# Layer 1 of a four-layer convolution stack: the residual folded into the convolution's weights, and the results' statistics taken on ScalarE

## The chip, the cores and the metric

One core of a Trainium2 chip runs the whole program. The time is device microseconds of one execution; a kernel's time is the median of its runs. The profile is one more execution, recorded by the hardware profiler. It is somewhat longer than the timed runs.

## The reference

Four layers run one after the other on x of 4 images, 64 channels, 256 x 256 points, in float32. Each is x + f(gn(x)), where gn normalises groups of two channels over the image. The change touches layer 1, whose f is a plain 3x3 convolution:

```python
def _gn(v, G=32, eps=1e-5):
    B_, C_, H_, W_ = v.shape
    g = v.reshape(B_, G, C_ // G, H_, W_)
    m = jnp.mean(g, axis=(2, 3, 4), keepdims=True)
    s = jnp.var(g, axis=(2, 3, 4), keepdims=True)
    return ((g - m) / jnp.sqrt(s + eps)).reshape(v.shape)

# --- layer 1 (conv_preact) ---
x = x + _L1_conv_ref(_gn(x), L1_conv_kernel)   # 3x3, 64 -> 64 channels, padding 1
```

Layer 0 is a gated depthwise convolution with 8x8 Fourier patches, layer 2 a convolution that chooses between two results point by point, layer 3 a Fourier filter. Each layer needs the mean and variance of the whole image that the layer before wrote, so each layer also collects statistics of its own results for the next.

## The kernel before

Layers run in order; between them x goes through device memory (one tensor for each image). Each layer is written as a loop over steps in which the order of the instructions on TensorE (PE), VectorE (DVE), ScalarE (ACT) and SyncE (SP, which issues the loads) is the order in which the code calls its functions (the block `manual_schedule`); GpSimd (POOL) issues the stores. At the seams between layers a scheduler may move the first work of the next layer ahead.

Layer 1 (`_layer1`, from L727) works in 64 steps: 4 images times 16 stretches of 16 rows. In a step n:

- `load` (L750) brings 2 x 10 rows: partitions 0 to 63 hold the channels of the upper 8 rows with a row on each side, partitions 64 to 127 those of the lower 8. The buffers of x come from `slot`, two for even and two for odd steps, so four in all.
- `normalize` (L772) writes gn(x) = r * x + nb with one ScalarE operation (L236) into one of two buffers xn. r (1/std) and nb (-mean/std) are known for each channel and image.
- `transform` (L788) forms four row combinations of xn on VectorE (L802). The convolution is a fast one along the rows: two output rows come from four products (index 0 to 3) instead of six.
- `product` (L804) computes product i on TensorE: for each of three column taps four matmuls of 64x64 weights with 512 points (L809), the four quarters of the array beside each other. Products 0 and 3 also add the residual, unnormalised x, with the identity matrix as weights (L817). The weights are `wk` for products 0 and 3, and `wg`, half the sum (or difference) of the three row taps, for 1 and 2.
- `fetch` (L822) copies product 1 from PSUM to SBUF on ScalarE (L824); `middle` (L826) forms product 1 plus and minus product 2 on VectorE (L830); `result` (L832) adds product 0 or 3 to these into the output tile o (L836, "o1", three buffers).
- `finish` (L840) takes bn_stats of o on VectorE (L849, four of 128x512 each step) and stores o (L852). After the last stretch of an image, `group_norm_parts` (L173) turns the statistics into r and nb of layer 2 in small pieces, one piece a step (`next_norms`): bn_aggr (L180), a matmul over the channel groups, a few small VectorE operations, a second matmul, a power on GpSimd.

The PSUM tiles of the products rotate over four buffers. Loads run three steps ahead, normalising two, transforming one; `finish` lies one step behind. The main loop reads:

```python
load(n + 3)
product(n, 1); fetch(n); product(n, 2)
finish(n - 1)
transform(n + 1, 1, 2); middle(n)
product(n, 0); result(n, 0)
transform(n + 1, 0, 3); normalize(n + 2)
product(n, 3); result(n, 3)
```

At the end of layer 1, layer 2 (`_layer2`, from L894) reuses the slots for its x and xn: its first normalised tiles are the input of its first convolve (L1044), which also needs constants (peri, thr, scl, wc) whose memory layer 1 held.

Of the kernel before, what the change touches and what calls it, by code (L numbers as in the profile page):

```python
# [10 lines left out]
F32 = mybir.dt.float32  # L11
U32 = mybir.dt.uint32
AF = mybir.ActivationFunctionType
ALU = mybir.AluOpType
# [3 lines left out]
C = 64  # L18
# [100 lines left out]
class _Net:  # L119
# [49 lines left out]
    def group_norm(self, *args):  # L169
        for _ in self.group_norm_parts(*args):  # L170
            pass

    def group_norm_parts(self, n, b, bst, avg=None):  # L173

        same, moved = avg or (self.avg, self.avg)
        nc, sp = self.nc, self.sp
        mv = sp.tile([128, 2], F32, tag="mv", name=f"mv{n}_{b}")
        nc.vector.bn_aggr(mv, bst.rearrange("p n s -> p (n s)"))  # L180
        yield
        ps = self.small(f"gn{n}_{b}")
        nc.tensor.matmul(ps[:, 0:1], same, mv[:, 0:1], start=True, stop=True)
        if moved is not same:
            nc.tensor.matmul(ps[:, 1:2], moved, mv[:, 0:1], start=True, stop=True)
        gm = sp.tile([128, 1], F32, tag="gm", name=f"gm{n}_{b}")
        nc.vector.tensor_copy(gm, ps[:, 0:1])
        d = sp.tile([128, 1], F32, tag="gd", name=f"gd{n}_{b}")
        nc.vector.tensor_sub(d, mv[:, 0:1], gm)
        q = sp.tile([128, 1], F32, tag="gq", name=f"gq{n}_{b}")  # L190
        nc.vector.scalar_tensor_tensor(q, d, d, mv[:, 1:2], ALU.mult, ALU.add)
        if moved is not same:
            nc.vector.tensor_copy(gm, ps[:, 1:2])
        yield
        ps2 = self.small(f"gv{n}_{b}")
        nc.tensor.matmul(ps2[:, 0:1], moved, q, start=True, stop=True)
        v = sp.tile([128, 1], F32, tag="gv", name=f"gvs{n}_{b}")
        nc.vector.tensor_scalar(v, ps2[:, 0:1], EPS, None, ALU.add)
        r, nb = self.r[n][:, b : b + 1], self.nb[n][:, b : b + 1]
        nc.gpsimd.tensor_tensor(r, v, self.mhalf, ALU.pow)  # L200
        nc.vector.scalar_tensor_tensor(nb, gm, -1.0, r, ALU.mult, ALU.mult)
# [525 lines left out]
    def _layer1(self, ctx, src, dst):  # L727
        tc, nc, a, B, H, W = self.tc, self.nc, self.a, self.B, self.H, self.W
        pool = lambda name, bufs, **k: ctx.enter_context(tc.tile_pool(name=name, bufs=bufs, **k))
        cp, p_t = pool("l1c", 1), pool("l1t", 2)  # L730
        p_s, p_o, pp = pool("l1s", 2), pool("l1o", 3), pool("l1p", 1, space=PSUM)
        turn = count()

        def pair(name):

            return pp.tile([128, 2, 512], F32, tag=f"p{next(turn) % 4}", name=name)

        self.small = lambda name: pair(name)[:, 0, :]
        rows2 = lambda t: t.rearrange("p s (r w) -> p s r w", r=2)
        W1 = W + 1  # L740
        halves = [slice(0, C), slice(C, 128)]

        xns = [self.slot(2, f"xn1_{k}")[:, 0:10] for k in range(2)]
        for t in xns:
            nc.gpsimd.memset(t[:, :, 0 : W + 2 : W1], 0.0)
        its = [(b, r0) for b in range(B) for r0 in range(0, H, 16)]
        NI = len(its)
        xt, ts, ms, sums, outs, bst = {}, {}, {}, {}, {}, {}

        def load(n):  # L750
            if n >= NI:
                return
            b, r0 = its[n]
            x = xt[n] = self.slot(n % 2, f"x1_{n}")[:, 0:10, 0:W]
            for s in range(2):
                top = r0 + 8 * s - 1
                i0, i1 = max(0, -top), min(10, H - top)
                nc.sync.dma_start(x[halves[s], i0:i1], src[b][:, top + i0 : top + i1, :])
# [7 lines left out]
        gs = [wk[:, 0]] + [cp.tile([128, 3, C], F32, name=f"wg{k}") for k in range(2)] + [wk[:, 2]]  # L766
        side = cp.tile([128, 3, C], F32, name="wside")
        nc.vector.tensor_add(side, wk[:, 0], wk[:, 2])
        for g, op in ((gs[1], nc.vector.tensor_add), (gs[2], nc.vector.tensor_sub)):
            op(g, side, wk[:, 1])  # L770
            nc.vector.tensor_scalar(g, g, 0.5, None, ALU.mult)  # L771
        def normalize(n):  # L772
            if n >= NI:
                return
            b, r0 = its[n]
            x, xn = xt[n], xns[n % 2]
            i0, i1 = 0, 10
            if r0 == 0:
                i0 = 1
                nc.gpsimd.memset(xn[0:C, 0, 1:W1], 0.0)  # L780
                self.normalize(xn[C:128, 0, 1:W1], x[C:128, 0], 1, b, C, 128)
            if r0 + 16 == H:
                i1 = 9
                nc.gpsimd.memset(xn[C:128, 9, 1:W1], 0.0)
                self.normalize(xn[0:C, 9, 1:W1], x[0:C, 9], 1, b, 0, C)
            self.normalize(xn[:, i0:i1, 1:W1], x[:, i0:i1], 1, b)

        def transform(n, *which):  # L788
            if n >= NI:
                return  # L790
            xn = xns[n % 2]
            if n not in ts:
                ts[n] = p_t.tile([128, 4, 4, W + 2], F32, tag="t", name=f"t_{n}")
            d = [xn[:, k : k + 7 : 2] for k in range(4)]
            for i in which:
                p, q, op = (
                    (d[0], d[2], nc.vector.tensor_sub),
                    (d[1], d[2], nc.vector.tensor_add),
                    (d[2], d[1], nc.vector.tensor_sub),
                    (d[3], d[1], nc.vector.tensor_sub),  # L800
                )[i]
                op(ts[n][:, i], p, q)  # L802

        def product(n, i):  # L804
            m = ms[n, i] = pair(f"m{i}_{n}")
            tiles = [(s, j) for s in range(2) for j in range(2)]
            for dx in range(3):
                for s, j in tiles:
                    nc.tensor.matmul(  # L809
                        rows2(m)[halves[j], s], gs[i][halves[s], dx, :],  # L810
                        ts[n][halves[s], i, 2 * j : 2 * j + 2, dx : dx + W],
                        start=(dx == 0), stop=(dx == 2 and i in (1, 2)),
                    )
            if i in (0, 3):
                r = 1 if i == 0 else 2
                for s, j in tiles:
                    nc.tensor.matmul(  # L817
                        rows2(m)[halves[j], s], self.ident[halves[s], halves[s]],
                        xt[n][halves[s], r + 4 * j : r + 4 * j + 3 : 2], start=False, stop=True,
                    )  # L820

        def fetch(n):  # L822
            t = sums[n, 1] = p_s.tile([128, 2, 512], F32, tag="s1", name=f"s1_{n}")
            nc.scalar.copy(t, ms.pop((n, 1)))  # L824

        def middle(n):  # L826
            m1, m2 = sums.pop((n, 1)), ms.pop((n, 2))
            for i, op in ((0, nc.vector.tensor_add), (3, nc.vector.tensor_sub)):
                t = sums[n, i] = p_s.tile([128, 2, 512], F32, tag=f"s{i}", name=f"s{i}_{n}")
                op(t, m1, m2)  # L830
# [9 lines left out]
        def finish(n):  # L840
            if n < 0:
                return
            b, r0 = its[n]
            if b not in bst:
                bst[b] = self.stats_tile(f"bst2_{b}", H * W // 1024)
            o = outs.pop(n)
            for s in range(2):
                for i in (0, 2):
                    nc.vector.bn_stats(bst[b][:, r0 // 4 + i + s, :], o[:, s, i : i + 2].rearrange("p r w -> p (r w)"))  # L849
            v = dst[b][:, r0 : r0 + 16, :].rearrange("c (s j r) w -> j c s r w", s=2, j=2)  # L850
            for j in range(2):
                nc.gpsimd.dma_start(v[j], o[halves[j]])  # L852
            if r0 + 16 == H:
                self.norms.append(self.group_norm_parts(2, b, bst.pop(b)))

        with tc.manual_schedule(
            engines={
                mybir.EngineType.PE, mybir.EngineType.DVE, mybir.EngineType.Activation, mybir.EngineType.SP
            }
        ):  # L860
            for n in range(2):
                normalize(n)
            transform(0, 1, 2, 0, 3)
            for n in range(NI):
                load(n + 3)
                product(n, 1)
                fetch(n)
                product(n, 2)
                finish(n - 1)
                transform(n + 1, 1, 2)  # L870
                middle(n)
                product(n, 0)
                result(n, 0)
                transform(n + 1, 0, 3)
                normalize(n + 2)
                product(n, 3)
                result(n, 3)
                self.next_norms()
                xt.pop(n)
                ts.pop(n)  # L880
            finish(NI - 1)

# [496 lines left out]
```

## Time and profile before

| | before |
|---|---|
| time, median of 3 runs | 7563.33 us (7562.54 to 7565.89) |
| span of the profiled execution | 7617.3 us |
| mean granted TensorE clock | 0.971 |
| TensorE matmul / weight load busy | 7303.1 / 4319.0 us |
| VectorE busy | 6594.7 us |
| ScalarE busy | 3659.3 us |
| GpSimd busy | 660.3 us |
| layer 1, first to last matmul | about 4886 to 5660 us |

A view of groups names a line, an engine, an operation, what is written from what, the shape, how many there were, their busy time and mean duration, and the idle time of that engine just before them with what ended it. A chain of waits follows the end of the program back from each instruction to what released it. A view in order of time merges equal neighbours. Matmuls overlap: four that use different quarters of the array run together, so their durations don't add up.

### The profile page before, as it was taken

What the parts mean: (1) busy time and instruction counts of PE and PEld (TensorE: products, weight loads), DVE (VectorE), ACT (ScalarE), POOL (GpSimd) and SP (SyncE); (2) the same over time, 40 slices, a digit from 0 to 9 for tenths busy, and PEclk for the clock granted to TensorE, in tenths of its full rate; (3) what the DMA queues carried; (4) which work ended last, traced back from release to release, by engine and by line L of the source; (5) the groups of instructions that cost most, each with busy time, mean ns of one, the idle gap of its engine ahead of it and who ended that gap; (6) DMA issues with size and microseconds to landing.
All of it is one profiled execution on the core that took longest, in us unless ns stands there. A gap on an engine that the chain in (4) does not pass through costs nothing. (4 is left out here: it accounts for less than half of the span.)

```text
span 7617.3 us, 398890 instructions
## 1 busy us (share of the span) xinstructions
PE 7303.1 (96%) x189304; PEld 4319.0 (57%) x189304; DVE 6594.7 (87%) x5915; ACT 3659.3 (48%) x3917; POOL 660.3 (9%) x1435
## 2 busy tenths in 40 slices
PE   6999999999999999999999999899989999998797
PEld 4666666666666666666666666433324444443276
DVE  7999999999999999999899899899989888885345
ACT  3445444444444454444444545322238778774111
POOL 0000000000000000000000000001102222221011
PEclk9999999999999999999999999999999999999955
DMA  3222222222222222222111121487766766677789
GB/s 129 62 65 63 63 61 61 59 61 59 61 62 61 59 59 62 62 59 54 45 47 47 46 50 44 100 197 196 195 162 171 178 171 175 171 178 232 243 333 396
DMA packets 651203, 875.63 MB, mean 115 GB/s; under 512 B 44020, under 2 KB 470212, under 8 KB 647524
## 3 DMA queue, kind: packets, MB, share of 16 engines
q1 hardware_dynamic: 568548, 581.61, 28.8%
q0 software_dynamic: 81024, 268.50, 12.1%
q8 instruction: 1485, 24.33, 1.4%
q14 instruction: 146, 1.20, 0.1%
HBM read 581.50 MB, written 268.44 MB: 112 GB/s over the span
## 5 line engine op out<-in xcount | busy, mean ns | idle before, releaser
L462 PE MATMUL psd<-y,diag 32*32 32x512 f32 x73296 | 2547.8, 598 | 16.0 <-issue 14.5
L500 DVE SCALAR_TENSOR_TENSOR v<-y,sb_w_dw,v 128x2048 f32<-128x2048 f32 x1024 | 2391.0, 2335 | 110.3 <-ACT v L498 87.7
L462 PEld LDWEIGHTS psd<-y,diag 32*32 32x32 f32 x73296 | 1524.3, 103 | 877.9 <-issue 366.7
L442 ACT COPY y<-psy 128x512 f32<-128x512 f32 x1536 | 915.4, 659 | 1683.3 <-PE psy L435 1681.2
L400 DVE TENSOR_TENSOR up<-psu,flt 128x768 f32<-128x768 f32 x1024 | 932.4, 951 | 226.6 <-PE psu L397 225.8
L435 PEld LDWEIGHTS psy<-sb_c_bdft,up 64*64 64x64 f32 x49152 | 859.5, 135 | 350.9 <-issue 139.1
L435 PE MATMUL psy<-sb_c_bdft,up 64*64 64x64 f32 x49152 | 931.3, 221 | 32.6 <-issue 29.7
L397 PE MATMUL psu<-win,xf 64*64 64x384 f32 x8192 | 788.5, 487 | 18.5 <-DVE h L482 10.1
L1000 DVE TENSOR_TENSOR q<-xn 128x2313 f32<-128x2313 f32 (+2 forms) x256 | 627.3, 2493 | 1.7 <-ACT xn L236 1.7
L1055 PE MATMUL one<-z,wp 32*32 32x512 f32 x16384 | 592.6, 596 | 20.3 <-issue 15.4
L1001 ACT ACTIVATE q<-q 128x2313 f32<-128x2313 f32 (+2 forms) x256 | 528.9, 2086 | 32.0 <-DVE q L1000 30.7
L476 ACT ACTIVATE h<-psd 128x1024 f32<-128x1024 f32 x258 | 251.3, 1023 | 534.9 <-PE psd L462 534.9
L236 ACT ACTIVATE xn<-x,nb,r 128x1024 f32<-128x1024 f32 (+3 forms) x272 | 488.1, 1798 | 41.5 <-DVE q L1000 23.6
L1055 PEld LDWEIGHTS one<-z,wp 32*32 32x32 f32 x16384 | 366.5, 103 | 228.5 <-issue 87.4
L1014 PE MATMUL div<-q,ones 64*32 64x512 f32 x8192 | 469.0, 597 | 13.6 <-ACT q L1001 9.8
L407 POOL MEMSET y<- 128x22 f32 x384 | 52.2, 137 | 4251.2 <-ACT y L415 3217.2
L397 PEld LDWEIGHTS psu<-win,xf 64*64 64x64 f32 x8192 | 305.6, 134 | 184.6 <-issue 85.2
L1088 POOL DMA_DIRECT2D x<-r x512 | 274.2, 543 | 971.0 <-DVE r L1085 943.6
L809 PE MATMUL m<-t,wk 64*64 64x512 f32 x3072 | 352.5, 588 | 0.0
L809 PE MATMUL m<-t,wg 64*64 64x512 f32 x3072 | 343.5, 591 | 4.5 <-DVE wg L771 4.5
L1014 PEld LDWEIGHTS div<-q,ones 64*32 64x32 f32 x8192 | 153.6, 107 | 321.1 <-issue 256.9
L824 ACT COPY s<-m 128x1024 f32<-128x1024 f32 x64 | 64.8, 1013 | 558.9 <-PE m L809 548.6
(138 smaller groups left out, 7625.2 us busy)
## 6 DMA issues: line engine op xcount, KB each, us to landing
x<-x SPq DMA_DIRECT2D x240, 640.0 KB, 6.3
x<-x SPq DMA_DIRECT2D x122, 1024.0 KB, 10.7
x<-in_x_dram SPq DMA_DIRECT2D x256, 256.0 KB, 3.8
x<-o POOLq DMA_DIRECT2D x128, 512.0 KB, 9.2
r<-x SPq DMA_DIRECT2D x512, 128.0 KB, 4.1
x<-r POOLq DMA_DIRECT2D x512, 128.0 KB, 4.0
out_dram<-x POOLq DMA_DIRECT2D x64, 1024.0 KB, 9.8
r<-in_x_dram SPq DMA_DIRECT2D x248, 256.0 KB, 3.8
```

What stands on the lines that cost most here:

```text
L236: self.nc.scalar.activation(dst, src, AF.Identity, bias=self.nb[n][p0:p1, b : b + 1], scale=self.r[n][p0:p1, b : b + 1])
L397: nc.tensor.matmul(ps[halves[n], s, 0:384], xf[t][halves[s], n, 4 * g + k], win[halves[s]], start=True, stop=True)
L400: nc.vector.tensor_mul(ups[t, g][:, :, k, :], ps[:, :, 0:384], flt.broadcast_to([128, 2, 384]))
L435: nc.tensor.matmul(ps[halves[c], n, s, :, k, :], up[halves[n], s, k, i * 128 + c * C : i * 128 + (c + 1) * C], bdft[halves[n]], start=True ...
L442: nc.scalar.copy(yt[t][i][:, 3:11, w0 : w0 + 64].rearrange("p r (k n w) -> p n r k w", k=4, n=2), ps[:, :, s])
L462: ins = nc.tensor.matmul(d[q // 2][quarters[j], q % 2], diag[quarters[q], i, k, :], rows_in(t, i, quarters[q], j, dy)[:, :, dx : dx + W], ...
L500: nc.vector.scalar_tensor_tensor(v, s, wdw[:, 2, k : k + 1], v, ALU.mult, ALU.add)
L809: nc.tensor.matmul(rows2(m)[halves[j], s], gs[i][halves[s], dx, :], ts[n][halves[s], i, 2 * j : 2 * j + 2, dx : dx + W], start=(dx == 0), ...
L1000: nc.vector.tensor_sub(d, p0, p1)
L1001: nc.scalar.activation(d, d, AF.Square)
L1014: ins = nc.tensor.matmul(ps[quarters[j], h], ones[halves[h]], q[n, g, k][halves[h], r + 2 * j : r + 2 * j + 2, o : o + W], start=(m == 0), ...
L1055: ins = nc.tensor.matmul(rows2(ps[g])[quarters[j], k], w[quarters[i]], z[quarters[i], h, 2 * j + dy : 2 * j + dy + 2, dx : dx + W], tile_p ...
```

## The change

For layer 1 the residual x can be written with the normalised rows: x = std * gn(x) + mean, with std = 1/r and mean = -nb/r. So x + conv(gn(x)) is one convolution whose centre tap has std added on the diagonal, plus a constant for each channel. In the fast convolution the centre row tap lies in products 1 and 2 only: half of std is added to the centre column's weights of product 1 and taken from those of product 2. The constant goes in as a bias where product 1 is fetched. The matmuls with the identity are dropped; so x is no longer held until they have run.

For each image `fold` computes std, mean and the two changed 64x64 weights on VectorE, where that image's first normalize is called.

The statistics of the results move from VectorE (bn_stats) to ScalarE: two passes over o, one for the sum of o and one for the sum of (o - c) squared, c being the mean of the image's first stretch; both write the values themselves to a tile that nobody reads (`junk`). `sums_parts` makes mean and variance of them at the image's end. At the first stretch of an image VectorE computes c from the first sum.

```diff
+    def sums_parts(self, n, b, acc, c, size):
+        def aggregate(mv):
+            t = sp.tile([128, 2], F32, tag="sums", name=f"sums{n}_{b}")
+            nc.vector.tensor_reduce(t, acc.rearrange("p k s -> p s k"), mybir.AxisListType.X, ALU.add)
+            nc.vector.tensor_scalar(t, t, 1.0 / size, None, ALU.mult)
+            nc.vector.tensor_copy(mv[:, 0:1], t[:, 0:1])
+            d = sp.tile([128, 1], F32, tag="sumd", name=f"sumd{n}_{b}")
+            nc.vector.tensor_add(d, t[:, 0:1], c)
+            nc.vector.tensor_mul(d, d, d)
+            nc.vector.tensor_sub(mv[:, 1:2], t[:, 1:2], d)
+        return self.group_norm_parts(n, b, aggregate)
...
+        half = cp.tile([128, C], F32, name="half")
+        for s in range(2):
+            nc.vector.tensor_scalar(half[halves[s]], self.ident[halves[s], halves[s]], 0.5, None, ALU.mult)
+        junk = cp.tile([128, 2, 4, W], F32, name="junk")
+
+        def fold(b):
+            r = self.r[1][:, b : b + 1]
+            t = p_i.tile([128, 2], F32, tag="i", name=f"i_{b}")
+            nc.vector.reciprocal(t[:, 0:1], r)
+            nc.vector.scalar_tensor_tensor(t[:, 1:2], self.nb[1][:, b : b + 1], -1.0, t[:, 0:1], ALU.mult, ALU.mult)
+            w = p_i.tile([128, 2, C], F32, tag="w", name=f"wi_{b}")
+            nc.vector.scalar_tensor_tensor(w[:, 0], half, t[:, 0:1], gs[1][:, 1], ALU.mult, ALU.add)
+            nc.vector.tensor_scalar(w[:, 1], half, t[:, 0:1], None, ALU.mult)
+            nc.vector.tensor_sub(w[:, 1], gs[2][:, 1], w[:, 1])
+            folded[b] = t[:, 1:2], w
+
         def normalize(n):
...
-            x, xn = xt[n], xns[n % 2]
+            x, xn = xt.pop(n), xns[n % 2]
             i0, i1 = 0, 10
             if r0 == 0:
                 i0 = 1
+                fold(b)
...
         def product(n, i):
             m = ms[n, i] = pair(f"m{i}_{n}")
-            tiles = [(s, j) for s in range(2) for j in range(2)]
+            w = [gs[i][:, dx] for dx in range(3)]
+            if i in (1, 2):
+                w[1] = folded[its[n][0]][1][:, i - 1]
             for dx in range(3):
...
-            if i in (0, 3):
-                r = 1 if i == 0 else 2
-                for s, j in tiles:
-                    nc.tensor.matmul(
-                        rows2(m)[halves[j], s], self.ident[halves[s], halves[s]],
-                        xt[n][halves[s], r + 4 * j : r + 4 * j + 3 : 2], start=False, stop=True,
-                    )
 
         def fetch(n):
             t = sums[n, 1] = p_s.tile([128, 2, 512], F32, tag="s1", name=f"s1_{n}")
-            nc.scalar.copy(t, ms.pop((n, 1)))
+            nc.scalar.activation(t, ms.pop((n, 1)), AF.Identity, bias=folded[its[n][0]][0])
...
             o = outs.pop(n)
-            for s in range(2):
-                for i in (0, 2):
-                    nc.vector.bn_stats(bst[b][:, r0 // 4 + i + s, :], o[:, s, i : i + 2].rearrange("p r w -> p (r w)"))
+            k = r0 // 16
+            if k == 0:
+                acc[b] = self.sp.tile([128, H // 16, 2], F32, tag="acc", name=f"acc_{b}")
+            nc.scalar.activation(junk, o, AF.Identity, accum_out=acc[b][:, k, 0:1])
+            if k == 0:
+                acc["c", b] = self.sp.tile([128, 1], F32, tag="accc", name=f"accc_{b}")
+                nc.vector.tensor_scalar(acc["c", b], acc[b][:, 0, 0:1], -1.0 / (8 * W), None, ALU.mult)
+            nc.scalar.activation(junk, o, AF.Square, bias=acc["c", b], accum_out=acc[b][:, k, 1:2])
...
             if r0 + 16 == H:
-                self.norms.append(self.group_norm_parts(2, b, bst.pop(b)))
+                self.norms.append(self.sums_parts(2, b, acc.pop(b), acc.pop(("c", b)), H * W // 2))
...
-                xt.pop(n)
                 ts.pop(n)
```

More of the change, by code (lines that the diff above doesn't have):

```diff
@@ L171, in group_norm @@
             pass
+    def sums_parts(self, n, b, acc, c, size):
+        nc, sp = self.nc, self.sp
+        def aggregate(mv):
[8 more added lines that the diff above has]
+        return self.group_norm_parts(n, b, aggregate)
     def group_norm_parts(self, n, b, bst, avg=None):
@@ L179, in group_norm_parts @@
         mv = sp.tile([128, 2], F32, tag="mv", name=f"mv{n}_{b}")
-        nc.vector.bn_aggr(mv, bst.rearrange("p n s -> p (n s)"))
+        if callable(bst):
+            bst(mv)
+        else:
+            nc.vector.bn_aggr(mv, bst.rearrange("p n s -> p (n s)"))
         yield
@@ L731, in _layer1 @@
         p_s, p_o, pp = pool("l1s", 2), pool("l1o", 3), pool("l1p", 1, space=PSUM)
+        p_i = pool("l1i", 2)
         turn = count()
@@ L747, in _layer1 @@
         NI = len(its)
-        xt, ts, ms, sums, outs, bst = {}, {}, {}, {}, {}, {}
+        xt, ts, ms, sums, outs, acc, folded = ({} for _ in range(7))
         def load(n):
@@ L805, in product @@
             m = ms[n, i] = pair(f"m{i}_{n}")
-            tiles = [(s, j) for s in range(2) for j in range(2)]
+            w = [gs[i][:, dx] for dx in range(3)]
+            if i in (1, 2):
+                w[1] = folded[its[n][0]][1][:, i - 1]
             for dx in range(3):
-                for s, j in tiles:
[L809 to L812, printed above, removed]
-                    )
-            if i in (0, 3):
-                r = 1 if i == 0 else 2
-                for s, j in tiles:
-                    nc.tensor.matmul(
-                        rows2(m)[halves[j], s], self.ident[halves[s], halves[s]],
-                        xt[n][halves[s], r + 4 * j : r + 4 * j + 3 : 2], start=False, stop=True,
-                    )
+                for s in range(2):
+                    for j in range(2):
+                        nc.tensor.matmul(
+                            rows2(m)[halves[j], s], w[dx][halves[s]],
+                            ts[n][halves[s], i, 2 * j : 2 * j + 2, dx : dx + W],
+                            start=(dx == 0), stop=(dx == 2),
+                        )
         def fetch(n):
             t = sums[n, 1] = p_s.tile([128, 2, 512], F32, tag="s1", name=f"s1_{n}")
-            nc.scalar.copy(t, ms.pop((n, 1)))
+            nc.scalar.activation(t, ms.pop((n, 1)), AF.Identity, bias=folded[its[n][0]][0])
         def middle(n):
@@ L843, in finish @@
             b, r0 = its[n]
-            if b not in bst:
-                bst[b] = self.stats_tile(f"bst2_{b}", H * W // 1024)
             o = outs.pop(n)
-            for s in range(2):
-                for i in (0, 2):
-                    nc.vector.bn_stats(bst[b][:, r0 // 4 + i + s, :], o[:, s, i : i + 2].rearrange("p r w -> p (r w)"))
+            k = r0 // 16
[6 more added lines that the diff above has]
+            nc.scalar.activation(junk, o, AF.Square, bias=acc["c", b], accum_out=acc[b][:, k, 1:2])
             v = dst[b][:, r0 : r0 + 16, :].rearrange("c (s j r) w -> j c s r w", s=2, j=2)
```

## The prediction

> **What bounds the kernel now.** I read the chain that ended last, then the groups of layer 1, then the order of time per engine, then the DMA share, then the seam to layer 2. The chain in two steady steps (start us, duration us, what):
>
> ```profile
> 4900.20 7.72 PE m L809 x72
> 4907.92 0.86 PE m L817 x8
> 4908.78 2.57 PE m L809 x24
> 4911.35 0.86 PE m L817 x8
> 4912.21 7.72 PE m L809 x72
> ```
>
> It is TensorE alone. A step (16 rows of the image) takes 4912.21 - 4900.20 = 12.01 us: 96 conv matmuls and 16 residual ones (L817). The trace has two matmul instructions for each call, so L817's x1024 are 64 steps x 8 calls x 2. The two L817 pieces are 2 x 0.86 = 1.72 us of each step. The groups of 4890 to 5650 us (count | busy us, mean ns | idle before and its releaser):
>
> ```profile
> L802 DVE TENSOR_TENSOR t<-xn 128x1032 f32<-128x1032 f32 x251 | 296.6, 1223 | 0.0
> L836 DVE TENSOR_TENSOR o<-m,s 128x1024 f32<-128x1024 f32 x126 | 154.0, 1222 | 14.7 <-PE m L817 14.7
> L849 DVE BATCH_NORM_STATS2 bst<-o 128x6 f32<-128x512 f32 x249 | 153.8, 680 | 1.9
> L830 DVE TENSOR_TENSOR s<-s,m 128x1024 f32<-128x1024 f32 x126 | 147.7, 1213 | 2.9 <-PE m L809 2.9
> L824 ACT COPY s<-m 128x1024 f32<-128x1024 f32 x63 | 63.8, 1013 | 548.6 <-PE m L809 548.6
> L236 ACT ACTIVATE xn<-x,nb,r 128x2560 f32<-128x2560 f32 x55 | 139.3, 2532 | 0.0
> ```
>
> VectorE hardly waits, so it is the close second; ScalarE waits most of the time. One step of VectorE in order of time (the bracket is idle before), then ScalarE's wait in a step:
>
> ```profile
> 5205.30 2.36 DVE L802 TENSOR_TENSOR t<-xn 128x1032 f32<-128x1032 f32 x2
> 5207.58 2.34 DVE L830 TENSOR_TENSOR s<-s,m 128x1024 f32<-128x1024 f32 x2
> 5210.24 1.23 DVE L836 TENSOR_TENSOR o<-m,s 128x1024 f32<-128x1024 f32 x1 [0.32 <-PE m L817]
> 5214.93 2.47 DVE L849 BATCH_NORM_STATS2 bst<-o 128x6 f32<-128x512 f32 x4
> 5217.32 2.36 DVE L802 TENSOR_TENSOR t<-xn 128x1032 f32<-128x1032 f32 x2
> ```
>
> ```profile
> 5216.30 1.01 ACT L824 COPY s<-m 128x1024 f32<-128x1024 f32 x1 [8.58 <-PE m L809]
> ```
>
> From start to start: a transform costs 1.14 us (2.28 for two), the four bn_stats 5217.32 - 5214.93 = 2.39. The stretch as a whole (busy of PE, PEld, DVE, ACT, POOL; then granted clock, DMA share, GB/s):
>
> ```profile
> 4886.00:5652.00 766.00, 766.00 (x7108) 274.56 (x7112) 742.04 (x777) 220.71 (x135) 78.95 (x140) 1.00 0.79 192
> ```
>
> TensorE is full at full clock, VectorE 97% busy, DMA 79%. SyncE's waits say why loads are not earlier: a buffer of x is held until the residual matmul has read it.
>
> ```profile
> SPq L758 <- PE m L817: 651.7, 60, 24.2
> ```
>
> Last, the seam:
>
> ```profile
> 5665.02 10.32 DMA x<-x
> 5675.37 0.05 issue
> 5675.42 2.53 ACT xn L236
> 5677.95 0.04 issue
> 5677.99 4.76 PE psz L1044 x23
> ```
>
> Layer 1's matmuls end near 5660.2; layer 2's first convolve runs from 5677.99, 17.8 us later, behind a load that had waited for an x buffer held by L817.
>
> **What the Trainium skill says.** (1) "ScalarE: Activation LUTs", section "What ACT_TABLE_LOAD costs": about 186 ns + 0.833 ns per element for an ACTIVATE with immediates, some 93 ns more for each pointer operand. The trace agrees: 128x2056 Square 1.92 us (1.90 by the page), 128x2560 normalize with two pointers 2.53 (2.50), L498 128x2048 with one 2.01 (1.99). (2) "ScalarE activation tables: per-element evaluation and per-set limits", section "What a function is on this engine": with the accumulator output and the same operands an instruction costs the same whatever the table. No row of before has an accumulator output. (3) "VectorE: DVE Perf Modes", section "Two Vector instructions with no wait between them": an op with an accumulator output is two instructions, the second an accumulator read. That is VectorE's; I take it as a warning for ScalarE. (4) "TensorE: Matmul & The Clock Gate", section "The mechanism": matmuls at different tile positions overlap. The trace agrees: 588 ns each, yet 8 in 0.86 us.
>
> **The change part by part.**
> Residual matmuls go. Each step has 96 instead of 112 matmul instructions at 12.01/112 = 0.1073 us: 10.30 us. 64 x 1.717 = 109.9 us, all on the path if nothing else exceeds 10.30. The replaced centre weights have the same shape: nothing on TensorE.
>
> bn_stats go. VectorE's step is 4 transforms and 2 sums at 1.14, 2 results at about 1.2, bn_stats 2.39: 11.6 us. After: 9.2, below 10.30. Had they stayed, VectorE would hold the step at 11.6, so they are needed for the gain. The cycle closes: the middle sums wait for product 2 (5.15 us into the step), end at 7.4; result 0 waits for product 0 (7.73), ends 8.9; transforms to 11.2; result 3 to 12.4; next transforms to 14.7; next sums at 15.45. VectorE has 0.75 us over.
>
> ScalarE gets two passes of 128x2048: Identity at 1.90 (immediates), Square with a bias pointer 2.01 (the L498 row). The accumulator read is unseen: between nothing and 0.3 us (the fixed part of a small ACTIVATE by page 1); I take 0.15. The fetch with a bias is 1.11 (L1031, 128x1024 from PSUM). Sum: 1.11 + 2.53 + 3.91 + 0.3 = 7.9 us of 10.30. Queued behind the passes is normalize(n+2): fetch starts at 2.6, passes end 6.9, normalize 9.4; VectorE wants it at 12.4. Hidden.
>
> A new wait: at the first step of each image VectorE waits for ScalarE's first sum (the shift). Its turn comes at 2.1, the sum is there at about 5.8; behind it stand the transforms for n+1, done 8.3 where TensorE wants them at 10.3, and sums, done 10.6 where product 2 wants the buffer at 12.9. No TensorE wait; four times only.
>
> The folding (5 small VectorE operations an image, 0.1 to 0.2 us each) and the last sums (6 small ones instead of a 1.88 us bn_aggr) fit VectorE's spare time. At layer 1's start three small operations precede the first matmul, but two transforms that stood ahead of it move behind the weights: nothing.
>
> x is released by normalize instead of the residual: loads may run about three steps earlier. Nothing waited for them in steady state, so no gain; DMA share becomes 0.79 x 12.01/10.30 = 0.92.
>
> Seam. In the built order layer 2's second normalize stands ahead of fetch(62), behind a load freed by normalize(63) and eight loads of r. SyncE takes 8.7 us for those (from the timeline), then the x load lands after 6 to 8 us: ScalarE is held until about 10 us into step 62, and the fetch ends 3.3 us after TensorE wanted the buffer: +3. In exchange layer 2's load is there early; its start then waits for ScalarE's last two passes (1.2 + 4 us after the matmuls), then constants (about 5 us): some 10.5 instead of 17.8: -7. Together -4, between -9 and +5.
>
> Sum: -109.9 - 4 = -114. The saved matmuls do not depend on profiling, so 7563.3 - 114 = 7449 us.
>
> **The rivals.**
> A, TensorE stays the bound: 7449.
> B, DMA becomes the bound. The queues' packets need 0.79 x 12.01 = 9.5 us a step. If this mix of 1 KB rows and stores cannot exceed about 0.85, a step takes 11.17 us: 54 + 4 saved, 7505. Against: 20 us slices of the stretch already reach nine tenths, and layer 3's end runs at 411 GB/s and full share. For: layer 1 has never run at 0.92 on average.
> C, the ScalarE passes cost about double (3.8 us): 1.1 + 2.5 + 7.6 = 11.2 us a step, or a spoilt normalize: 52 saved, about 7507. Against: the page's constant price and the L498 row.
> D, slower: Identity and Square turn out to need different tables. Two loads a step at 1.283 us (the trace's row) and by page 1 some 1.38 us of drain each, 5.3 us: ScalarE 7.9 + 5.3 = 13.2 us, 64 x 1.2 = 76 longer, 7640. Against: layer 2 alternates Identity and Square and the trace has only two table loads in all.
>
> **How the numbers follow.** A 0.84, B 0.07, C 0.05, D 0.04. 7449 is A's. A's spread is the seam, 7440 to 7458, with a little for lost TensorE time at image borders and DMA contention, up to 7475. Half of B and C lies higher and is left out with D: range 7436 to 7480. Faster by over 0.2% (15 us): A and nearly all of B and C, 0.94; same 0.02; slower 0.04.
>
> **What would show it.** In the profile after: L817 gone, TensorE's product lines in an unbroken chain with 10.3 us a step; VectorE waiting about 1 us a step for TensorE; ScalarE's two passes near 1.9 and 2.0 us; DMA share near 0.92 in the stretch; a gap to layer 2's first convolve of about 10 us; one TensorE wait of some 3 us in the last two steps. I am wrong if TensorE waits each step on a transform, a buffer or a load, if the passes exceed 3 us, or if the clock falls below 1.00 there.

## The result, and the profile after

| | before | after |
|---|---|---|
| time, median | 7564.61 us (7562.54 to 7572.59, 4 runs) | 7466.28 us (7464.03 to 7472.07, 4 runs) |
| ratio, 95% interval | | 0.9869 (0.9852 to 0.9886) |
| span of the profiled execution | 7617.3 us | 7469.9 us |
| layer 1, first to last matmul | 4886.0 to 5660.2: 774.2 us | 4846.5 to 5522.0: 675.5 us |
| layer 1's last matmul to layer 2's first full convolve | 17.8 us | 10.3 us |
| layer 1's first matmul to the end | 2731.3 us | 2623.4 us |

The changed kernel is 98 us faster. The profiles differ by more, 147 us, but 39.5 us of that lie ahead of layer 1 (4886.0 against 4846.5), in layer 0, where the change does nothing; the profiled execution of before was also 54 us longer than its timed runs. So I measure from layer 1's first matmul to the end, where the two differ by 107.9 us: 105.6 up to layer 2's first periphery matmul (the table of the experiments has the pieces) and 2.3 behind it.

The chain of waits over some three steady steps of layer 1, after the change (start us, duration us, what), is one unbroken piece (L852 is the line of the matmuls that was L809):

```profile
4999.82 30.45 PE m L852 x281
```

TensorE still sets the pace, and the pieces of L817 that stood between those of the convolution are gone. The groups of 4890 to 5545 us (count | busy us, mean ns | idle before and its releaser), to be held against those of before:

```profile
L842 DVE TENSOR_TENSOR t<-xn 128x1032 f32<-128x1032 f32 x237 | 280.7, 1227 | 0.0
L872 DVE TENSOR_TENSOR o<-m,s 128x1024 f32<-128x1024 f32 x121 | 147.8, 1221 | 8.5 <-PE m L852 8.5
L866 DVE TENSOR_TENSOR s<-s,m 128x1024 f32<-128x1024 f32 x120 | 141.1, 1217 | 52.2 <-PE m L852 36.7 <-ACT s L860 15.4
L888 ACT ACTIVATE junk<-o,accc 128x2048 f32<-128x2048 f32 x61 | 122.2, 2004 | 2.5 <-DVE accc L887 0.7
L884 ACT ACTIVATE junk<-o 128x2048 f32<-128x2048 f32 x61 | 116.1, 1903 | 5.3 <-DVE o L872 3.8 <-DVE gm L207 1.5
L860 ACT ACTIVATE s<-m,i 128x1024 f32<-128x1024 f32 x60 | 66.8, 1114 | 154.7 <-PE m L852 154.7
L884 ACT ACTIVATION_READ_ACCUMULATOR junk<-o 128x1 f32 x61 | 11.6, 190 | 0.0
```

VectorE now waits ahead of the middle sums (L866), mostly for TensorE, where it hardly waited before; ScalarE's idle time ahead of the fetch falls from 548.6 to 154.7 us and is filled with the two passes, 1.90 and 2.00 us, each with an accumulator read of 0.19. One step of ScalarE in order of time:

```profile
5306.49 1.11 ACT L860 ACTIVATE s<-m,i 128x1024 f32<-128x1024 f32 x1 [2.75 <-PE m L852]
5307.50 1.90 ACT L884 ACTIVATE junk<-o 128x2048 f32<-128x2048 f32 x1
5309.30 0.19 ACT L884 ACTIVATION_READ_ACCUMULATOR junk<-o 128x1 f32 x1
5309.52 2.00 ACT L888 ACTIVATE junk<-o,accc 128x2048 f32<-128x2048 f32 x1
5311.44 0.19 ACT L888 ACTIVATION_READ_ACCUMULATOR junk<-o,accc 128x1 f32 x1
5311.53 2.51 ACT L256 ACTIVATE xn<-x,nb,r 128x2560 f32<-128x2560 f32 x1
```

It works 5314.04 - 5306.49 = 7.55 us of the step and waits 2.75 for the next product. The stretches of layer 1 as a whole and of one step (busy of PE, PEld, DVE, ACT, POOL; then granted clock, DMA share, GB/s):

```profile
4846.50:5522.00 675.50, 665.88 (x6156) 238.21 (x6156) 596.23 (x562) 480.74 (x388) 78.75 (x140) 0.99 0.90 220
5300.00:5310.30 10.30, 10.30 (x100) 3.67 (x96) 9.28 (x10) 7.51 (x7) 1.18 (x2) 1.00 0.91 225
```

In the step TensorE is busy throughout at full clock, with DMA at 0.91. Over the whole layer it is idle 675.50 - 665.88 = 9.6 us. The chain of waits at the end of layer 1 shows where:

```profile
5481.46 13.20 DMA r<-x
...
5496.65 9.73 DMA x<-x
...
5506.49 0.07 ACT xn L256
...
5508.92 1.10 ACT s L860
5510.02 0.04 issue
5510.06 11.94 PE m L852 x96
5522.00 0.02 issue
...
5530.31 1.85 DMA wc<-in_core_dram
5532.17 0.14 issue
5532.30 4.37 PE psz L1082 x16
```

Read upwards from 5510.06: the last step's 96 matmuls wait for a fetch (L860), that stands on ScalarE behind a normalize of layer 2 (L256), that waits for a load of x, that SyncE could issue only behind layer 2's eight loads of r. Below it is the second wait of the seam: the first convolve (L1082) follows on the load of the constant wc.

### The profile page after: what moved, and what is told of

The parts are those of the page before. It is cut to its first block, busy times and chain, and to the rows that moved or that the text cites. A ratio compares the mean times of both kernels' runs of the same rounds, so it can differ in the third digit from the quotient of the medians.

```text
span 7469.9 us, 396764 instructions
## 1 busy us (share of the span) xinstructions
PE 7164.3 (96%) x188280; PEld 4283.8 (57%) x188280; DVE 6440.8 (86%) x5705; ACT 3917.9 (52%) x4173; POOL 658.6 (9%) x1435
## 3 DMA queue, kind: packets, MB, share of 16 engines
q0 software_dynamic: 81024, 268.50, 12.4%
## 5 line engine op out<-in xcount | busy, mean ns | idle before, releaser
L1093 PE MATMUL one<-z,wp 32*32 32x512 f32 x16384 | 594.6, 597 | 17.6 <-issue 13.1
L256 ACT ACTIVATE xn<-x,nb,r 128x1024 f32<-128x1024 f32 (+3 forms) x272 | 487.1, 1794 | 28.3 <-DMA x<-x 24.4
L1093 PEld LDWEIGHTS one<-z,wp 32*32 32x32 f32 x16384 | 366.9, 103 | 226.4 <-issue 84.6
L852 PE MATMUL m<-t,wk 64*64 64x512 f32 x3072 | 341.1, 588 | 0.0
L535 DVE TENSOR_TENSOR v<-g,v 64x1024 f32<-64x1024 f32 x257 | 313.5, 1220 | 9.3 <-ACT g L528 1.4
L502 DVE TENSOR_TENSOR h<-h,psd 128x1024 f32<-128x1024 f32 x258 | 302.7, 1215 | 6.1 <-PE psd L482 5.7
```

What stands on the lines that cost most here:

```text
L256: self.nc.scalar.activation(dst, src, AF.Identity, bias=self.nb[n][p0:p1, b : b + 1], scale=self.r[n][p0:p1, b : b + 1])
L852: nc.tensor.matmul(rows2(m)[halves[j], s], w[dx][halves[s]], ts[n][halves[s], i, 2 * j : 2 * j + 2, dx : dx + W], start=(dx == 0), stop=(d ...
L1093: ins = nc.tensor.matmul(rows2(ps[g])[quarters[j], k], w[quarters[i]], z[quarters[i], h, 2 * j + dy : 2 * j + dy + 2, dx : dx + W], tile_p ...
```

## The experiments

Each run below was timed in one of four groups, beside runs of before on the same chip; before's own median differs from group to group (7564.61, 7600.61, 7591.01, 7587.20 us). Layer 0 takes a different time in each execution, so the table gives the piece of the profile that the change can reach, layer 1's first matmul to the end, beside the medians. All columns but the last two are read from profiles, in us. A periphery matmul is one of the many that write the tile `one` in layer 2's loop (L1055 before, L1093 after).

| kernel | start of the program to layer 1's first matmul | layer 1, first to last matmul | layer 1's last matmul to layer 2's first periphery matmul | layer 1's first matmul to the end | median us | median of before beside it |
|---|---|---|---|---|---|---|
| before | 4886.0 | 774.2 | 52.8 | 2731.3 | 7564.61 | |
| after | 4846.5 | 675.5 | 45.9 | 2623.4 | 7466.28 | 7564.61 |
| after_again | 4878.9 | 676.5 | 45.5 | 2624.5 | 7492.67 | 7600.61 |
| e3_seam | 4873.0 | 664.1 | 45.4 | 2617.7 | 7492.76 | 7600.61 |
| e7_seam_consts | 4851.0 | 663.9 | 37.4 | 2608.9 | 7458.34 | 7600.61 |
| e2_stats_only | 4869.7 | 774.6 | 49.9 | 2721.6 | 7592.64 | 7600.61 |
| e1_fold_only | 4865.2 | 755.0 | 41.2 | 2701.2 | 7569.45 | 7591.01 |
| e4_square_twice | 4865.1 | 680.3 | 46.8 | 2624.1 | 7491.34, one run | 7591.01 |
| e5_square_thrice | 4869.9 | 749.9 | 64.3 | 2717.6 | 7589.67, one run | 7591.01 |
| after_third | 4863.5 | 677.5 | 45.9 | 2624.8 | 7491.14 | 7587.20 |
| e9_consts_only | 4859.0 | 676.0 | 37.6 | 2614.5 | 7468.75 | 7587.20 |
| e8_paced | 4847.6 | 664.4 | 38.0 | 2601.6 | 7459.80 | 7587.20 |
| e6b_no_shift | 4848.2 | 677.5 | 45.6 | 2637.8 | 7488.07, one run | 7587.20 |

**The yardstick.** The changed kernel without an edit.

> The changed kernel once more, as the yardstick of this group. My account of the measured 98 us: layer 1 itself gives 64 x 1.717 = 110 us, TensorE then waits some 10 us in the last step, the seam to layer 2 gives back 7. So about 7466 us, with layer 1 from first to last matmul near 675 us (before 774) and 10.3 us from its last matmul to layer 2's first convolve (before 17.8). Rival (DMA takes the rest of the gain): the same time, but layer 1 would lose it in every step, over 10.4 us each.

> The changed kernel once more as the yardstick of this group: about 0.987 of before; from layer 1's first matmul to the end 2624 us, layer 1 itself 676 us. If layer 0, which the change doesn't touch, is what moves the totals from one execution to the next, its length will differ from the 4846 and 4879 us of the two profiles so far, while the 2624 us stay within 2.

Ratios to before 0.9856 (0.984 to 0.9872) and 0.9877 (0.986 to 0.9893). Layer 1 to the end agrees within 1.4 us over three executions (2623.4, 2624.5, 2624.8), while layer 0 took 4846.5, 4878.9 and 4863.5 us in the same program. The account holds: TensorE waits 10.36 and 9.78 us in the last step in these two executions (9.57 in the first), and the loss is at the end.

**Each half of the change alone.** First the folded residual with bn_stats left on VectorE:

```diff
-            nc.scalar.activation(junk, o, AF.Identity, accum_out=acc[b][:, k, 0:1])
...
-            nc.scalar.activation(junk, o, AF.Square, bias=acc["c", b], accum_out=acc[b][:, k, 1:2])
+            for s in range(2):
+                for i in (0, 2):
+                    nc.vector.bn_stats(bst[b][:, r0 // 4 + i + s, :], o[:, s, i : i + 2].rearrange("p r w -> p (r w)"))
```

> The changed kernel with the old statistics: the residual is folded into the weights, bn_stats stay on VectorE. Theory (VectorE is the close second: 11.6 us of work a step): layer 1's steps take about 11.5 to 11.7 us instead of 12.01, TensorE waits for VectorE in every step, the total is only 25 to 35 us below before. Rival (the matmuls alone bring the gain, VectorE's statistics fit in the gaps): 10.3 us a step and about 108 us below before.

VectorE in order of time, in a step of this kernel:

```profile
5200.49 2.36 DVE L841 TENSOR_TENSOR t<-xn 128x1032 f32<-128x1032 f32 x2
5202.77 2.35 DVE L865 TENSOR_TENSOR s<-s,m 128x1024 f32<-128x1024 f32 x2
5205.03 1.22 DVE L871 TENSOR_TENSOR o<-m,s 128x1024 f32<-128x1024 f32 x1
5206.17 2.37 DVE L841 TENSOR_TENSOR t<-xn 128x1032 f32<-128x1032 f32 x2
5208.45 1.22 DVE L871 TENSOR_TENSOR o<-m,s 128x1024 f32<-128x1024 f32 x1
5209.70 2.47 DVE L884 BATCH_NORM_STATS2 bst<-o 128x6 f32<-128x512 f32 x4
5212.09 2.36 DVE L841 TENSOR_TENSOR t<-xn 128x1032 f32<-128x1032 f32 x2
```

There is no idle time left on VectorE: it works through the whole step, 5212.09 - 5200.49 = 11.60 us. Layer 1 to the end is 30.1 us shorter than before (expected 25 to 35); the medians give 21.6 us, ratio 0.9978 (0.9967 to 0.9988), a little less than expected. Without the residual matmuls VectorE is the bound.

Second, only the statistics moved; the identity matmuls and the code of product and fetch stay as before, `finish` and `sums_parts` are those of the change:

```diff
-            for s in range(2):
-                for i in (0, 2):
-                    nc.vector.bn_stats(bst[b][:, r0 // 4 + i + s, :], o[:, s, i : i + 2].rearrange("p r w -> p (r w)"))
...
+            nc.scalar.activation(junk, o, AF.Identity, accum_out=acc[b][:, k, 0:1])
...
+            nc.scalar.activation(junk, o, AF.Square, bias=acc["c", b], accum_out=acc[b][:, k, 1:2])
```

> The kernel before with only the statistics moved to ScalarE; the residual stays as matmuls. Theory (TensorE sets the step): a step stays at 12.01 us, VectorE waits about 2.4 us a step more, the total is within 5 us of before (7560 to 7570; the seam may move it a little). Rival (VectorE set the pace, or a share of it): 20 us or more faster. Rival (two passes on ScalarE cost the path something each step): slower by over 10 us.

Measured: a layer 1 of 774.6 us against 774.2, and a step in which TensorE is full:

```profile
5200.00:5212.02 12.02, 12.02 (x116) 4.28 (x112) 9.30 (x9) 7.43 (x6) 1.19 (x3) 1.00 0.81 202
```

VectorE's work of a step falls to 9.30 us and nothing comes of it in layer 1. The total is 8 us below before (0.999, 0.9981 to 0.9999), a little outside what I expected. In the profile it is 9.7 us from layer 1 on: 2.9 at the seam and 7.2 in layers 2 and 3, where I did not look for a cause and where other kernels scatter as much. So I compare up to layer 2's first periphery matmul alone: 774.2 + 52.8 = 827.0 us before, 796.2 with the folded residual, 824.5 with the statistics moved, 721.4 with both. The parts are worth 31 and 3 us alone and 106 together: each takes away one of two bounds that lie 0.4 us apart (12.01 and 11.60 us a step).

**How hidden the passes on ScalarE are.** Its Square pass done twice, then three times:

```diff
             nc.scalar.activation(junk, o, AF.Square, bias=acc["c", b], accum_out=acc[b][:, k, 1:2])
+            nc.scalar.activation(junk, o, AF.Square, bias=acc["c", b], accum_out=acc[b][:, k, 1:2])
```

> The changed kernel with ScalarE's second pass (Square) done twice: 2.0 us more on ScalarE in each step, 9.6 in all. Theory (ScalarE's work is hidden behind TensorE's 10.3 us): layer 1's steps stay at 10.30 us, layer 1 grows by the last step's passes alone, under 5 us from layer 1's first matmul to the end of the program (2624 us in the changed kernel). Rival (the passes cost the path something in each step, since normalize is queued behind them): over 20 us.

> The changed kernel with the Square pass done three times: 11.6 us on ScalarE in each step. Theory: now ScalarE sets the step, 11.6 us instead of 10.30, some 80 to 90 us from layer 1's first matmul to the end. Rival (ScalarE's passes are hidden whatever their length, as nothing in the step waits for the sums): no change.

Twice: the step stays at 10.30 us, so the 2 us per step, 128 us of work, are hidden in the steps. Layer 1 is some 4 us longer (680.3 against 675.5 to 677.5), as its last wait grew to 13.85 us. That the total from layer 1 on is 2624.1 us, as without the edit, owes to a layer 2 that happened to be as much shorter. Three times, ScalarE from fetch to fetch:

```profile
5202.24 1.09 ACT L860 ACTIVATE s<-m,i 128x1024 f32<-128x1024 f32 x1
5203.24 1.90 ACT L884 ACTIVATE junk<-o 128x2048 f32<-128x2048 f32 x1
...
5211.52 2.51 ACT L256 ACTIVATE xn<-x,nb,r 128x2560 f32<-128x2560 f32 x1
5213.93 1.09 ACT L860 ACTIVATE s<-m,i 128x1024 f32<-128x1024 f32 x1
```

The wait ahead of the fetch is gone, and a step is 5213.93 - 5202.24 = 11.69 us. From layer 1 on the program takes some 93 us more (2717.6 against 2623.4 to 2624.8): 73 in layer 1 and 18 in the seam, where ScalarE is still at its last passes. That is the 64 x (11.69 - 10.30) = 89 of the steps, though not all of it falls within layer 1's matmuls: TensorE no longer waits in the last step, and ScalarE ends later than it. Between 9.6 us of work (free) and 11.6 (it sets the step) lies TensorE's 10.30.

**The new wait at an image's start.** The sum of squares is taken without c (and `sums_parts` no longer corrects for it):

```diff
-            if k == 0:
-                acc["c", b] = self.sp.tile([128, 1], F32, tag="accc", name=f"accc_{b}")
-                nc.vector.tensor_scalar(acc["c", b], acc[b][:, 0, 0:1], -1.0 / (8 * W), None, ALU.mult)
-            nc.scalar.activation(junk, o, AF.Square, bias=acc["c", b], accum_out=acc[b][:, k, 1:2])
+            nc.scalar.activation(junk, o, AF.Square, accum_out=acc[b][:, k, 1:2])
```

> The changed kernel with the sum of squares taken of o itself, without c, so that VectorE doesn't wait for ScalarE's first sum at an image's start. Theory (that wait, 3 us four times, is used up by VectorE's spare time): layer 1 within 2 us of 676. Rival (the wait delays the transforms and TensorE with them): layer 1 shorter by 8 to 14 us.

In the changed kernel VectorE does wait for the first sum, as its line in the waits of layer 1 shows (us in total, times, longest):

```profile
DVE accc L887 <- ACT junk L884: 11.4, 4, 3.5
```

Without it layer 1 takes 677.5 us, as the yardstick beside it does. The four waits cost nothing. This run was longer by 13 us after the seam, in layer 2's loop, which the edit doesn't touch; that stays unexplained.

**The wait in the last step.** First by dealing layer 2's x buffers out otherwise:

```diff
-                xt[n, g] = self.slot(((2 * n + g) % 3) % 2, f"x2_{n}_{g}")[:, 0:10, 0:W]
+                xt[n, g] = self.slot(((2 * n + g) % 3) // 2, f"x2_{n}_{g}")[:, 0:10, 0:W]
```

> The changed kernel, with layer 2's x buffers dealt out otherwise: the load that layer 2's second normalize needs takes the buffer freed one step earlier, so it is issued ahead of the eight loads of r. My theory (ScalarE was held by that load, and TensorE waited 9.6 us for the fetch behind it): the TensorE wait goes, layer 1 shrinks from about 675 to about 664 us, the total falls by 10 to 12 us, to about 7455. Rival (the shortfall lies in DMA contention or in layer 0, not in this wait): layer 1 still near 675, total within 3 us of 7466.

The wait goes and layer 1 falls to 664.1 us, 12.4 less than the yardstick of its group. But of this only 6.8 us are left at the end of the program, and the medians are equal (7492.76 and 7492.67), so the total was missed. In the profile layer 2's loop, first to last periphery matmul, takes 1264.1 us with the new buffers (1264.3 in e7_seam_consts) against 1258.2, 1260.4 and 1257.5 in the three executions of the changed kernel. Against its own yardstick (1260.4) 3.7 us are given back there and 2.0 behind that loop. The scatter of the loop among other kernels, 1254.9 to 1271.3, is wider, so this is a possible cause and not a shown one.

Then with the constants of layer 2 loaded early as well, into memory of their own:

```diff
+        self.consts2 = [cp.tile([128, k], F32, name=f"sb_{n}") for n, k in (("peri", 8), ("thr", 1), ("scl", 1), ("wc", C))]
...
+        for t, name in zip(self.consts2, ("peri", "thr", "scl")):
+            nc.sync.dma_start(t, a[name])
+        for s in range(2):
+            nc.sync.dma_start(self.consts2[3][halves[s]], a["core"])
...
-        peri, thr, scl = self.load("peri", cp), self.load("thr", cp), self.load("scl", cp)
+        peri, thr, scl, wc = self.consts2
```

> As e3, and layer 2's four small constants get memory of their own and are loaded at the start of layer 1. Theory: in the changed kernel layer 2's first convolve waits for them, since their memory is freed only when ScalarE's last pass is done; with them early the convolve starts right after layer 1's last matmul, the squares of the differences about 7 us sooner: total about 7 us below e3, near 7448. Rival (layer 2's start is set by ScalarE's last two passes or by the differences on VectorE alone): 0 to 2 us below e3.

And the constants alone:

> The changed kernel with layer 2's constants loaded early into memory of their own, which also shifts all tiles behind them; the seam's loads and buffers as they are. Theory: layer 1 still 676 us with its wait, the seam 7 to 9 us shorter, so about 2616 us from layer 1's first matmul to the end; layer 0 somewhere between 4845 and 4890 us as in every run. Rival (the moved memory makes layer 0 faster, which the run with both edits suggested): layer 0 near 4850 us in profile and time, and the total 25 us or more below the changed kernel.

The early constants shorten the seam by 8 us in both (45.4 to 37.4, 45.9 to 37.6), as expected. The medians fall by more: 34.4 us from e3_seam to e7_seam_consts, 22.4 from the changed kernel to e9_consts_only, where the profiles from layer 1 on say 8.8 and 10.3. The rest is in layer 0 or in the scatter between executions. Layer 0's 4859.0 us in e9_consts_only is not the 4850 that its rival wanted. But all three kernels with the early constants show such a surplus (the one below falls by 31.3 us in the medians and 23.2 in the profile), so whether the shifted tiles make layer 0 faster stays open.

Last, order at the seam by two explicit waits, with the buffers as they were and the early constants:

```diff
-                load(n, g, s)
+                load(n, g, s, self.mark[62, 1] if (n, g) == (0, 1) else None)
...
-                load_r(0, 0, g)
+                load_r(0, 0, g, self.mark[63, 0])
```

(`mark` keeps the last matmul of each product.) The first wait lets SyncE issue the load only once step 62's product 1 is done; the second puts the loads of r behind it. So layer 2's normalize stands behind the fetch that TensorE waits for.

> The changed kernel with layer 2's seam put in order and its buffers left as they were: the load for layer 2's second normalize waits for step 62's product 1 and goes ahead of the loads of r (which wait for step 63's product 0), so that its normalize stands behind step 62's fetch on ScalarE; the four constants are loaded early. Theory: the TensorE wait of about 10 us in the last step goes (layer 1 about 664 us), the first convolve follows within 2 us, and layer 2's loop doesn't lose the 5 us that other buffers cost it: 2600 to 2606 us from layer 1's first matmul to the end, some 20 us less than the changed kernel. Rival (ScalarE or the loads move the wait to another place at the seam): less than 8 us.

The end of TensorE's layer 1 in order of time, first in the changed kernel, then here:

```profile
5495.16 5.33 PE L852 MATMUL m<-t,wk 64*64 64x512 f32 x48
5510.06 1.99 PE L852 MATMUL m<-t,wg 64*64 64x512 f32 x8 [9.57 <-ACT s L860]
...
5532.30 7.03 PE L1082 MATMUL psz<-xn,wc 64*64 64x512 f32 x40 [10.35 <-DMA wc<-in_core_dram]
```

```profile
5496.39 5.33 PE L858 MATMUL m<-t,wk 64*64 64x512 f32 x48
5501.54 1.04 PE L858 MATMUL m<-t,wg 64*64 64x512 f32 x8
...
5514.14 6.18 PE L1085 MATMUL psz<-xn,sb_wc 64*64 64x512 f32 x40 [2.12 <-DVE o L878]
```

Both waits are gone: 9.57 us ahead of the last step and 8 of the 10.35 ahead of the convolve. The eight loads of r, issued after those of x, now take SyncE 3.98 us. From layer 1 to the end it is 2601.6 us, 23.2 less than the changed kernel beside it (expected 2600 to 2606), 21 of them in layer 1 and the seam; the medians are 7459.8 and 7491.1 us, ratio to before 0.9833 (0.9818 to 0.9847) against 0.9877 (0.986 to 0.9893). Against e9_consts_only, which has the early constants alone, the two waits bring 12.9 us from layer 1 on. This version beats both kernels.

## Why the prediction was right, step by step

The prediction of 7449 us (114 saved) was right in its direction, its main mechanism and its range, and 17 us too low. That the time itself fell into 7436 to 7480 is in part luck: in the first group before took 7564.61 us, close to the 7563.33 that the prediction started from. In two later groups, with before at 7600.61 and 7587.20, the changed kernel took 7492.67 and 7491.14 us. What carries over is the difference: 98, 108 and 96 us against 114.

- **Residual matmuls, 109.9 us.** Right: 10.30 us a step, TensorE full at clock 1.00. (12.01/112 is 0.1072, not 0.1073; that moves a step by 0.01 us.) Layer 1 before is 64 x 12.01 = 769 and 5 us for its start and end; after, 64 x 10.30 = 659 and 16.
- **bn_stats must go too.** Right: with them the step is 11.60 us (e1_fold_only), the 11.6 of the prediction.
- **ScalarE's two passes, 7.9 us a step, hidden.** Right: 7.55 us, and 2 us more stay hidden. The prices of the Trainium skill's "ScalarE: Activation LUTs", section "What ACT_TABLE_LOAD costs", held: 1.90 and 2.00 us at 2048 elements. The accumulator read, taken at 0.15 us, is an instruction of its own and takes 0.19. Rivals C (passes of 3.8 us) and D (two table loads a step) are out: layer 1 has no table load. One working was wrong: a fetch that starts 2.6 us into the step and takes 1.11, then passes of 4.2, end at 7.9 and not 6.9, and the normalize at 10.4 and not 9.4, as in the step shown above (10.4 from that step's first matmul at 5303.67). VectorE wants it at 12.4, so it stays hidden.
- **The wait for c, fold and the last sums: nothing.** Right for the wait (e6b_no_shift); for the small operations only in that the step is unbroken.
- **DMA share 0.92.** Measured 0.90 in the layer and 0.91 in a step; with the last wait removed (e3_seam) the layer runs at 0.93:

```profile
4873.00:5537.10 664.10, 664.09 (x6156) 238.50 (x6156) 596.31 (x562) 480.66 (x388) 78.99 (x140) 1.00 0.93 224
```

That ends the rival in which this mix of transfers could not pass 0.85.
- **The seam, -4 us: the term that was mis-sized.** The mechanism was as described, the wait in the last step and the shorter way to the convolve. The second part was -7.5 (predicted -7). The first was about +11 (predicted +3): layer 1's surplus over 64 steps rose from 5 to 16 us. The fetch ended 9.6 us after TensorE could have gone on, where 3.3 had been worked out, and TensorE began again at about half speed (8 matmuls in 1.99 us instead of 1.04, at a granted clock of 0.50), some 1.6 us more. Two durations in that working were too short. SyncE's eight loads of r took 13.15 us and not 8.7 (before, then after):

```profile
5649.58 8.69 SPq L966 DMA_DIRECT2D r<-x  x8
5481.46 13.15 SPq L1004 DMA_DIRECT2D r<-x  x8
```

In both kernels the last of the eight goes out when the load of x issued just ahead of them has landed: that took 9.10 us before and 13.57 after. The DMA queues moved 234 GB/s while these loads of r went out before, and 280 after; that this is why the load took longer is likely and was not tested. The load of x behind them took 9.73 us and not 6 to 8. Here the prediction passed over its own line of the seam, in which that load takes 10.32 us. Nor was that load held by L817 to the last: L817's hold ended at 5648.2, and the chain shows the load behind a constant and a load of r that took 11.47 us to land. Together the seam gave +3.5 instead of -4.
- **What is left.** -109.9 + 11 - 7.5 = -106.4, against the profile's -107.9 from layer 1 on. The timed difference, 98 us in the first group, 108 and 96 in two others, differs from it by up to 12 us; the one part of the program that differs that much between executions of the changed kernel is layer 0. Profiling was said to leave the saved matmuls alone, which holds; but a total of this kernel cannot be predicted closer than layer 0's scatter.

## What to carry to other kernels

Where two engines run within a few per cent of each other, an edit that relieves one is worth only the distance to the other: here 31 and 3 us alone, 106 together. A pass moved to an engine with spare time is free as long as that engine's sum stays below the bound and sets the step beyond it (here at 9.6 and 11.6 us against 10.30), so add up that engine's step before moving. At a seam, look at what a scheduler moved ahead on an engine that works in the order of its code: here one early normalize waited 16.1 us for its load and held the fetch behind it, and two waits that set the order of the loads were worth 12.9 us.

## What the runs showed that I had not expected

- Layer 0 took 4846.5, 4878.9 and 4863.5 us in three executions of one program, with a granted clock of 0.99 to 1.00 from 70 to 4700 us. TensorE's waits in that stretch sum to 50, 61 and 60 us, of which the profile puts 25, 39 and 35 down to "issue", so they are only a part of the difference. The three executions belong to three groups, the last two on different chips, and before's median moves with them (7564.61, 7600.61, 7587.20 us); but within the second group the runs of before still spread from 7585.92 to 7617.87. How much is the chip and how much the execution was not separated, and the cause was not found.
- The accumulator output of a ScalarE pass is a second instruction of 0.19 us (185 to 197 ns over 64 of them).
- After 9.57 us without work, TensorE's first 8 matmuls took 1.99 us instead of 1.04; the granted clock was 0.50 in these 1.99 us.
- The same eight loads of r, 128 KB each, kept SyncE 8.69 us in before, 13.15 after the change, and 3.98 where the loads of x had landed ahead of them (e8_paced).
